# A decoder layer on one core: keys and values prepared one batch ahead, the experts' w2 product in seven block products, and three tiles for the decays

## The chip, the cores and the metric

The kernel is one program on one core of a Trainium2 chip, with float32 data throughout. The metric is the device time of one launch, in microseconds (us): 5657.23 as the median of three runs, 5656.19 to 5658.22. Five engines work side by side, each in its own order: PE multiplies matrices (a weight load and a multiplication by turns), DVE does elementwise work, reductions and scans, ACT does functions and scaled copies, POOL does the rest and issues the indirect transfers, and SP issues nearly all other transfers (DMA). SBUF is the on-chip memory, PSUM holds matmul results, and DRAM is the memory outside the core. An engine or SP that waits holds up what stands behind it in its own queue.

## The reference, cut to what matters

The input x has 8 batches of 512 tokens of 512 values. Three blocks follow each other, each as layernorm(x + block(x)).

```python
# 1. state space block: 1024 channels, 16 states a channel, along the tokens t
h[t] = exp(A * dt[t]) * h[t-1] + dt[t] * B[t] * x_main[t]
y[t] = sum over states of h[t] * C[t]
out  = ((y + x_main * D) * silu(z)) @ out_proj_w + x
# 2. cross attention, 16 heads of 32; keys and values come from ctx, not from x
q, k, v = x @ Wq.T + bq, ctx @ Wk.T + bk, ctx @ Wv.T + bv
out = softmax(q k.T / sqrt(32)) v @ Wo.T + bo
# 3. 32 experts, the best 4 for each token, 640 places each, and a shared expert
xe = xp[buf_tok].reshape(E, cap, DIM)
h = silu(xe @ w1) * (xe @ w3)
out = (h @ w2) * buf_w
y = zeros.at[buf_tok].add(out)
z = silu(xf @ sw1) * (xf @ sw3) @ sw2
return y + z
```

## The kernel before, in words

The program has three parts: `layers` (blocks 1 and 2, the shared expert and the choice of experts), `experts`, and `finish` (the last layernorm). The framework sets the order of every engine's instructions when the program is built, by their order in the source as a priority and by what it takes to be ready, and it places the waits. The order in the trace is therefore not the order of the source everywhere: an expert's weight sums, for instance, stand one expert earlier in DVE's order.

**The scan.** `layers` goes through 16 chunks: 8 batches of two chunks of 256 tokens. A chunk has 32 steps, each with 4 states of one group of 128 rows. In a step ACT writes the decays exp(A dt) into one of two tiles (`decays`, L434, four ACTIVATE), ahead by one step; `carry` (L440) puts the last state in front; DVE makes dt B x (L446), runs the recurrence (L450), and multiplies by C (`collect`, L467); PE sums over the states into `py` (L471). h has four buffers. The broadcasts of B and C, `bc`, come by SP's queue (L378) into four buffers. With the steps go the projections of the next chunk (L302) and the output projection of the last (`back`, L500), whose result is normed, written to DRAM as x1d (L512), and read again by `fetch` (L668).

**Beside the scan.** Attention and shared expert of the batch before are a list of small pieces with weights (`units(b)`), taken one by one between the steps of the scan, as a budget over both chunks allows. A piece issues its matmuls and leaves a second half (the copy out of PSUM) to be issued with the following piece. In batch 0 there are no such pieces; the pieces of batch 7 come after the last chunk, alone. A list begins with the loads of Wv, of ctx into `cT` and of the mask; then come four `values` products, copied by ACT into the value tile `va` (L690); four `keys` products, which DVE adds bk to and masks into `kT` (L702); the transposes of x1 (`flip`, L676); four `queries` products (L712). For every pair of heads `spread` copies rows of qT and kT into operand tiles (L722, L723). After attention come the output projection, a layernorm, the gate, the shared expert (`hidden`, `shared`) and the scatter of token rows to the experts' places (`send`, L638). Matmuls of this part have two PSUM tiles (tag `mm`) and weights two buffers (tag `wa`). Four large tiles are shared by tag: s1 holds x1T, then x2t; s2 holds cT, then attT; s3 holds qT, then hT; s4 holds kT, then x2T. Small rows of 512 values use two buffers with the tag `row`. During the first two chunks SP also clears the experts' token buffer, 43 MB in 32 transfers.

**The experts.** For each expert `load` fetches xe (1362.5 KB) and w1, w3, w2 (1024 KB each) into two buffers each. `hidden` computes silu(xe w1) * (xe w3) for two groups of 128 columns (r = 0, 1) and two halves of 320 tokens; its products with w1 and w3 are made as seven block products instead of eight, from sums of weight blocks (`sums_w`) and of token blocks (`sums_x`) that DVE makes (L1127, L1144 to L1147). `give` multiplies a tile of 128 tokens of hT by w2 (L1218: four matmuls of 128x512), ACT scales the result by the token's weight into y (L1222), and POOL adds it into `based` in DRAM by an indirect transfer (L1223). Five tiles make the 640 tokens; between them stand the transposes of the next expert's tokens (`flip`, L1136) and their copy (L1137). Each indirect transfer waits until the one before has landed, and the x load of the next expert but one into the same buffer waits for the last of them. PSUM has three tiles with the tag h, two with h2, one for transposes and two for L1218.

A matmul of 128x128 by N float32 columns is two records of N columns in the profile.

## Time and profile before

| | |
|---|---|
| median of 3 runs | 5657.23 us |
| profiled execution | 5660.41 us, of which the span from first to last instruction is 5658.7 us |
| PE, DVE, ACT, POOL busy in the span | 87%, 73%, 45%, 9% |
| granted clock of PE | 0.937 on average |
| scan with what goes beside it | to about 3724 us |
| last batch's attention and shared expert | 3724 to 3985 us |
| experts | 3985 to 5602 us, 49.5 us each |
| final layernorm | to the end |

In a row by stage the first pair of figures is the window and its length, then busy microseconds and instruction counts of PE, PEld (weight loads), DVE, ACT and POOL, the granted clock as a share of full speed, the mean share of time that the DMA engines worked, and GB/s. In a row of waits stand the engine and line that waited, what it waited for, the sum in us, how often, and the longest. In a row of the timeline stand the start, the duration of the merged group, engine and line, and in brackets the idle time before it with what ended it.

### The profile page before, as it was taken

The numbers are of one execution on the slowest core, as the hardware profiler recorded it, in microseconds if no ns is written. First come the engines' busy times: TensorE is split into PE (matmuls) and PEld (weight loads), VectorE is DVE, ScalarE is ACT, GpSimd is POOL, SyncE is SP. The second block draws the span as 40 slices with busy tenths as digits, with TensorE's granted clock in tenths as the row PEclk, the third lists the DMA queues.
The fourth block names the chain that finished last, engine by engine and source line by source line (L and its number), as shares of the span: only waits on it lengthen the run. The fifth ranks groups of instructions, "written<-read, shape, count | busy, mean of one in ns | idle before, by whom it ended". The sixth has DMA issues, their size and how long they took to land. (4 is left out here: it accounts for less than half of the span.)

```text
span 5658.7 us, 57578 instructions
## 1 busy us (share of the span) xinstructions
PE 4933.6 (87%) x18984; PEld 2576.2 (46%) x18984; DVE 4107.3 (73%) x5290; ACT 2548.5 (45%) x5347; POOL 525.2 (9%) x424
## 2 busy tenths in 40 slices
PE   5658889888988988988898898889899999999994
PEld 3334344334434433434443443333566666666662
DVE  5998988989899898898999999834444444444443
ACT  4454565654655456565465646513122222222223
POOL 0000001002000200200200020010211111111111
PEclk8778999999999999999999999999999999999997
DMA  7675345335433634544443363331544444444444
GB/s 205 192 225 176 96 127 164 110 116 158 137 105 108 188 95 127 162 112 117 159 136 105 110 194 94 107 110 43 159 123 115 118 125 115 119 117 123 115 118 137
DMA packets 484635, 744.49 MB, mean 132 GB/s; under 512 B 68170, under 2 KB 200810, under 8 KB 484336
## 3 DMA queue, kind: packets, MB, share of 16 engines
q1 hardware_dynamic: 446832, 655.52, 38.1%
q0 software_dynamic: 33280, 76.90, 7.1%
q10 hardware_dynamic: 4224, 8.39, 0.4%
q8 instruction: 150, 2.46, 0.2%
q14 instruction: 149, 1.22, 0.1%
HBM read 491.91 MB, written 148.28 MB: 113 GB/s over the span
## 5 line engine op out<-in xcount | busy, mean ns | idle before, releaser
L434 ACT ACTIVATE l_da<-both,l_aneg 128x256 f32<-128x256 f32 x2048 | 894.0, 499 | 837.6 <-DVE h L450 795.6
L450 DVE TENSOR_TENSOR_SCAN h<-l_da,h 128x1028 f32<-128x1028 f32 x512 | 1172.4, 2295 | 55.0 <-ACT h L440 28.7
L471 PE MATMUL py<-h,l_twice 128*64 128x256 f32 x4096 | 632.4, 421 | 225.9 <-DVE h L467 225.7
L446 DVE TENSOR_TENSOR h<-both,bc 128x1024 f32<-128x1024 f32 x512 | 619.5, 1217 | 125.2 <-PE py L471 58.3
L467 DVE TENSOR_TENSOR h<-h,bc 128x1024 f32<-128x1024 f32 x512 | 624.1, 1221 | 6.3 <-DVE l_state L452 0.3
L1218 PE MATMUL po<-w,hT 128*128 128x512 f32 x1280 | 575.1, 592 | 0.0
L471 PEld LDWEIGHTS py<-h,l_twice 128*64 128x64 f32 x4096 | 297.9, 147 | 588.1 <-DVE h L467 262.0
L735 PE MATMUL ps_s<-l_ka,l_qa 64*128 64x512 f32 x1024 | 316.9, 698 | 140.8 <-DVE mx L737 140.6
L1152 PE MATMUL ps_h<-xT,w 128*128 128x320 f32 x1536 | 436.7, 434 | 0.0
L1173 DVE TENSOR_TENSOR hT<-ps_h,p 128x320 f32<-128x320 f32 x128 | 63.0, 492 | 443.4 <-PE ps_h L1152 443.4
L1223 POOL DMA_INDIRECT based<-y,xe x160 | 252.2, 1576 | 1358.8 <-ACT y L1222 828.6
L737 DVE TENSOR_REDUCE mx<-ps_s 128x2 f32<-128x1024 f32 x256 | 310.9, 1217 | 81.6 <-PE ps_s L735 81.0
L1222 ACT ACTIVATE y<-po,xe 128x512 f32<-128x512 f32 x160 | 110.0, 688 | 551.7 <-PE po L1218 542.6
L1152 PEld LDWEIGHTS ps_h<-xT,w 128*128 128x128 f32 x1536 | 292.9, 191 | 131.8 <-issue 15.8
L1218 PEld LDWEIGHTS po<-w,hT 128*128 128x128 f32 x1280 | 231.1, 190 | 231.6 <-issue 224.1
L761 PE MATMUL ps_t<-l_qa,l_ka 64*128 64x512 f32 x1024 | 303.3, 655 | 12.9 <-ACT eT L765 9.0
L765 ACT ACTIVATE eT<-ps_t 128x1024 f32<-128x1024 f32 x256 | 258.9, 1013 | 108.3 <-PE ps_t L761 108.0
L777 PE MATMUL po<-eT,l_va 128*64 128x512 f32 x1024 | 278.8, 623 | 21.2 <-ACT raw L789 18.1
L1152 PE MATMUL ps_h<-t,s 128*128 128x320 f32 x1024 | 286.2, 432 | 0.0
L682 PE MATMUL ps_p<-x2T,wa 128*128 128x512 f32 x512 | 249.6, 639 | 21.1 <-DVE hT L852 19.2
L500 PE MATMUL po<-wm,zs 128*128 128x512 f32 x512 | 241.6, 623 | 21.5 <-DMA wm<-in_out_proj_w 21.5
L302 PE MATMUL ps_z<-xnT,wm 128*128 128x256 f32 x1024 | 241.6, 389 | 12.7 <-DMA wm<-in_in_proj_w 12.7
(205 smaller groups left out, 6695.3 us busy)
## 6 DMA issues: line engine op xcount, KB each, us to landing
bc<-scr SPq DMA_DIRECT2D x1024, 128.0 KB
w<-in_w SPq DMA_DIRECT2D x96, 1024.0 KB
wm<-in_in_proj_w SPq DMA_DIRECT2D x128, 512.0 KB
xbuf<-zero SPq DMA_DIRECT2D x32, 1362.5 KB
xe<-xbuf SPq DMA_DIRECT2D x32, 1362.5 KB
both<-dt SPq DMA_DIRECT2D x256, 128.0 KB
both<-dtx SPq DMA_DIRECT2D x256, 128.0 KB
wm<-in_out_proj_w SPq DMA_DIRECT2D x64, 512.0 KB
```

Source lines behind the costliest of these rows:

```text
L434: nc.scalar.activation(da[:, n, 1:], dt[:, c % 2, j, :], AF.Exp, scale=aneg[:, c, j, g, m : m + 1])
L446: nc.vector.tensor_tensor(steps, dtx[:, c % 2].unsqueeze(2).to_broadcast([P, 2, NG // 2, T]), bc[0], ALU.mult)
L450: nc.vector.tensor_tensor_scan(flat, da.rearrange("p n t -> p (n t)"), flat, 0.0, ALU.mult, ALU.add)
L467: nc.vector.tensor_tensor(steps, steps, bc[1], ALU.mult)
L471: nc.tensor.matmul(py[j * HP : (j + 1) * HP, c % 2, :], twice, h[:, j * 2 + m, 1:], start=False, stop=(s == (NST // NG - 1, NG // 2 - 1, 1)),)
L735: nc.tensor.matmul(ps[:, j, :], qa[r, lt * P : (lt + 1) * P], ka[r, :], start=True, stop=True)
L737: return lambda: nc.vector.tensor_reduce(mx[:, lt, :].unsqueeze(2), ps, AX.X, ALU.max) and None
L761: nc.tensor.matmul(ps[:, j, :], ka[r, kc * P : (kc + 1) * P], qa[r, :], start=True, stop=True)
L765: nc.scalar.activation(eT, ps, AF.Exp)
L777: nc.tensor.matmul(po[j * 2 * HD : (j + 1) * 2 * HD, :], va[:, kc, i, j * HD : (j + 2) * HD], eT[:, j, :], start=(kc == 0), stop=(kc == SC ...
L1152: nc.tensor.matmul(ps, w[:, n, r * P : (r + 1) * P], x[:, n, :], start=not more and n == 0, stop=n == 1, skip_group_check=more,)
L1218: nc.tensor.matmul(po, got["hT"][:, ic, j * P : (j + 1) * P], got["w2"][:, ic, :], start=(ic == 0), stop=(ic == DC - 1))
```

## The change

Three things are done.

First, keys and values move out of `units(b)` into a list of their own, `sources(b)`. The list for batch b+1 is run inside `units(b)` (its last two key products behind the start of `units(b)`), so during the scan of batch b+1; the list for batch 0 is run beside the scan of batch 0, which had nothing beside it; and `units(7)`, behind the last chunk, has none. The results are kept in DRAM (`kept`): a value or key product is copied into a `row` tile and stored by SP; `units` later loads the values into `va` by eight transfers in runs of 128 bytes, and `spread` loads key rows from DRAM instead of from kT. The tag s4 is gone; x2T goes into s3 and hT into s2. Wq is loaded at the first key product or, for the last batch, at the start of `units`.

Second, `give` now computes four of the five token tiles as two by two blocks (token halves of 256, column halves of 256, contraction halves of 256) with seven block products instead of eight; the fifth tile is computed as before. DVE makes four sums of w2's blocks (`sums_w2`, beside the first group of `hidden`) and four of hT's blocks (one of them in place). Partial results are scaled by the token's weight on ACT (`keep`), and DVE combines them (`use`). The transposes of the next expert are issued at five places between the products (`between`). hT, its sums and w2's sums have one buffer each, and y has seven.

Third, the decays have three tiles in turn instead of two.

Besides, two gate constants (`early`, `first`) are kept once and broadcast instead of stored four times, and two gate temporaries use a `row` tile.

```diff
-    das = [cp.tile([P, NG, T + 1], F32, name=f"l_da{i}") for i in range(2)]
+    das = [cp.tile([P, NG, T + 1], F32, name=f"l_da{i}") for i in range(3)]
...
+    early = cp.tile([P, E], F32, name="l_early")
...
+    early = early.unsqueeze(1).to_broadcast([P, SC, E])
...
+        both = p3.tile([P, D], F32, tag="row", name="g_eq").rearrange("p (n j g h) -> p n j g h", n=2, j=SC, g=G)
+        eq, gt = both[:, 0], both[:, 1]
...
+    kept = {}
+    def sources(b):
+        st, todo = {}, []
+        def begin():
             load("Wv")
             st["cT"] = cT = quad("s2", "cT")
             nc.sync.dma_start(cT, rows(a["ctx"][b]))
             st["mk"] = mk = p1.tile([P, S], U8, tag="mk", name="mk")
             nc.sync.dma_start(mk, a["mask"][b : b + 1, :].to_broadcast([P, S]))
+            kept[b] = [dp.tile([S, D], F32, tag="vd", name="vd"), dp.tile([D, S], F32, tag="kd", name="kd")]
+        def values(pc):
+            if pc == 0:
+                load("Wk")
+            w, cT = loaded["Wv"], st["cT"]
+            ps = dense(lambda dc: cT[:, dc, pc * P : (pc + 1) * P], lambda dc: w[:, dc, :])
+            def put():
+                v = p3.tile([P, D], F32, tag="row", name="v")
+                nc.scalar.copy(v, ps)
+                nc.sync.dma_start(kept[b][0][pc * P : (pc + 1) * P, :], v)
+            return put
+        def keys(oc):
+            if oc == 0 and b:
+                load("Wq")
+            w, cT = loaded["Wk"], st["cT"]
+            ps = dense(lambda dc: w[:, dc, oc * P : (oc + 1) * P], lambda dc: cT[:, dc, :])
+            def put():
+                k = p3.tile([P, D], F32, tag="row", name="k")
+                nc.vector.scalar_tensor_tensor(k, ps, bk[:, oc : oc + 1], st["mk"], ALU.add, ALU.mult)
+                nc.sync.dma_start(kept[b][1][oc * P : (oc + 1) * P, :], k)
+            return put
+        todo.append((0, begin, False))
+        for j in range(SC):
+            todo.append((3.4, lambda j=j: values(j), False))
+        for j in range(DC):
+            todo.append((3.4, lambda j=j: keys(j), False))
+        return todo
+    def dense(lhs, rhs):
+        ps = psm.tile([P, S], F32, tag="mm", name="ps_p")
+        for dc in range(DC):
+            nc.tensor.matmul(ps, lhs(dc), rhs(dc), start=(dc == 0), stop=(dc == DC - 1))
+        return ps
+    def units(b):
+        st = {}
+        todo = []
+        def begin():
+            if b == B - 1:
+                load("Wq")
             st["x1T"] = quad("s1", "x1T")
+            vd, st["kd"] = kept.pop(b)
+            for pc in range(SC):
+                for j in range(2):
+                    nc.sync.dma_start(
+                        va[:, pc, :, 2 * j * HD : (2 * j + 1) * HD],
+                        vd[pc * P : (pc + 1) * P, :].rearrange("p (i j d) -> p i j d", j=2, d=HD)[:, :, j, :],
+                    )
...
-        def values(pc):
-            if pc == 0:
-                load("Wk")
-            w, cT = loaded["Wv"], st["cT"]
-            ps = dense(lambda dc: cT[:, dc, pc * P : (pc + 1) * P], lambda dc: w[:, dc, :])
-            return lambda: nc.scalar.copy(
-                va[:, pc].rearrange("p i (j d) -> p i j d", d=HD)[:, :, 0:3:2, :],
-                ps.rearrange("p (i j d) -> p i j d", j=2, d=HD),
-            ) and None
-        def keys(oc):
-            if oc == 0:
-                load("Wq")
-                st["kT"] = quad("s4", "kT")
-            w, cT = loaded["Wk"], st["cT"]
-            ps = dense(lambda dc: w[:, dc, oc * P : (oc + 1) * P], lambda dc: cT[:, dc, :])
-            return lambda: nc.vector.scalar_tensor_tensor(
-                st["kT"][:, oc, :], ps, bk[:, oc : oc + 1], st["mk"], ALU.add, ALU.mult
-            ) and None
...
-                nc.sync.dma_start(ka[r1 : r1 + HD, :], st["kT"][r0 : r0 + HD, i // 2, :])
+                h0 = (2 * i + j) * HD
+                nc.sync.dma_start(ka[r1 : r1 + HD, :], st["kd"][h0 : h0 + HD, :])
...
-                st["x2T"] = quad("s4", "x2T")
+                st["x2T"] = quad("s3", "x2T")
...
-                st["hT"] = quad("s3", "hT")
+                st["hT"] = quad("s2", "hT")
...
-        for j in range(SC):
-            add(3.4, values, j)
-        for j in range(DC):
-            add(3.4, keys, j)
-            if j == 2:
-                add(0, fetch, 0)
+        more = sources(b + 1) if b + 1 < B else []
+        todo += more[:-2]
+        add(0, begin)
+        add(0, fetch, 0)
+        todo += more[-2:]
...
-        if t == 0 and b:
-            side, spent = units(b - 1), 0.0
+        if t == 0:
+            side, spent = units(b - 1) if b else sources(0), 0.0
...
-                decays(2 * nq + ni, ng, (f if k + 1 < len(steps) else nf)["ready", nq][0], das[(n + 1) % 2])
-            scan(t, 2 * q + ci, g, f["ready", q][1], bc, das[n % 2], h)
+                decays(2 * nq + ni, ng, (f if k + 1 < len(steps) else nf)["ready", nq][0], das[(n + 1) % 3])
+            scan(t, 2 * q + ci, g, f["ready", q][1], bc, das[n % 3], h)
...
+    def BW(w, j, k):
+        return w[:, 2 * j : 2 * j + 2, k * FH : (k + 1) * FH]
...
-        s1, s2, s4 = (wp.tile([P, 2, FH], F32, tag=f"{n}s{i}", name="s") for i in (1, 2, 4))
+        s1, s2, s4 = (wp.tile([P, 2, FH], F32, tag=f"{n}s{i}", name="s", bufs=1 if n == "hT" else 2) for i in (1, 2, 4))
...
+    def sums_w2(got):
+        w = got["w2"]
+        got["t2"] = t1, t2, t3, t4 = [wp.tile([P, 2, FH], F32, tag=f"w2t{i}", name="t", bufs=1) for i in range(4)]
+        for o, x, y in (
+            (t1, BW(w, 0, 1), BW(w, 0, 0)),
+            (t2, BW(w, 1, 1), t1),
+            (t3, BW(w, 1, 1), BW(w, 0, 1)),
+            (t4, BW(w, 1, 0), t2),
+        ):
+            nc.vector.tensor_tensor(o, x, y, ALU.subtract)
+            yield
...
-    def give(e, got, j):
-        xe = got["x"]
+    def give(e, got, side):
+        xe, hT, w2 = got["x"], got["hT"], got["w2"]
+        t1, t2, t3, t4 = got["t2"]
+        both = range(2)
+        ys = [p2.tile([P, D], F32, tag="y", name="y", bufs=CJ + 2) for j in range(CJ)]
+        def weight(j):
+            return xe[:, j, D + e : D + e + 1]
+        def keep(ps, r, tag, j):
+            v = p2.tile([P, HALF], F32, tag=f"{tag}{r}", name=tag)[:, 0:FH]
+            nc.scalar.activation(v, ps, AF.Identity, scale=weight(j))
+            return v
+        def use(j, k, ps, more):
+            nc.vector.scalar_tensor_tensor(ys[j][:, k * FH : (k + 1) * FH], ps, weight(j), more, ALU.mult, ALU.add)
+        def put(j):
+            nc.gpsimd.indirect_dma_start(
+                out=based,
+                out_offset=bass.IndirectOffsetOnAxis(ap=xe.bitcast(I32)[:, j, D + E :], axis=0),
+                in_=ys[j],
+                in_offset=None,
+                bounds_check=N + P - 1,
+                compute_op=ALU.add,
+            )
+        for _ in sums_w(got, "hT"):
+            pass
+        s1, s2, s3, s4 = got["hT", "s"]
+        next(side, None)
+        xs, p1, pu, p5 = [], [], [], []
+        for r in both:
+            xs.append(psx.tile([P, HALF], F32, tag="h", name="ps_o")[:, 0:FH])
+            product(xs[r], A(hT, 0, 0), r, BW(w2, 0, 0))
+            p1.append(keep(xs[r], r, "p1", r))
+        j = CJ - 1
         po = pso.tile([P, D], F32, tag="po", name="po")
         for ic in range(DC):
-            nc.tensor.matmul(
-                po, got["hT"][:, ic, j * P : (j + 1) * P], got["w2"][:, ic, :], start=(ic == 0), stop=(ic == DC - 1)
-            )
-        y = p2.tile([P, D], F32, tag="y", name="y", bufs=CJ + 1)
-        nc.scalar.activation(y, po, AF.Identity, scale=xe[:, j, D + e : D + e + 1])
-        nc.gpsimd.indirect_dma_start(
-            out=based,
-            out_offset=bass.IndirectOffsetOnAxis(ap=xe.bitcast(I32)[:, j, D + E :], axis=0),
-            in_=y,
-            in_offset=None,
-            bounds_check=N + P - 1,
-            compute_op=ALU.add,
-        )
+            nc.tensor.matmul(po, hT[:, ic, j * P : (j + 1) * P], w2[:, ic, :], start=(ic == 0), stop=(ic == DC - 1))
+        nc.scalar.activation(ys[j], po, AF.Identity, scale=weight(j))
+        put(j)
+        next(side, None)
+        for r in both:
+            ps = psy.tile([P, HALF], F32, tag="h2", name="ps_o")[:, 0:FH]
+            product(ps, A(hT, 0, 1), r, BW(w2, 1, 0))
+            use(r, 0, ps, p1[r])
+        for r in both:
+            product(xs[r], s2, r, t2, more=True)
+            pu.append(keep(xs[r], r, "pu", r))
+        next(side, None)
+        zs = []
+        for r in both:
+            zs.append(psy.tile([P, HALF], F32, tag="h2", name="ps_o")[:, 0:FH])
+            product(zs[r], s1, r, t1)
+            p5.append(keep(zs[r], r, "p5", 2 + r))
+        for r in both:
+            product(xs[r], s3, r, t3, more=True)
+            use(2 + r, 1, xs[r], p5[r])
+        next(side, None)
+        for r in both:
+            product(zs[r], s4, r, BW(w2, 1, 1), more=True)
+            use(r, 1, zs[r], pu[r])
+            put(r)
+        next(side, None)
+        for r in both:
+            product(xs[r], A(hT, 1, 1), r, t4, more=True)
+            nc.scalar.activation(ys[2 + r][:, 0:FH], xs[r], AF.Identity, scale=weight(2 + r))
+            put(2 + r)
+    def between(nxt):
+        sums = sums_w(nxt, "w3")
+        for j in range(CJ):
+            flip(nxt, j)
+            if j == CJ - 1:
+                sums_x(nxt)
+            next(sums, None)
+            yield
...
-        got["hT"] = p2.tile([P, DC, CAP], F32, tag="hT", name="hT")
+        got["hT"] = p2.tile([P, DC, CAP], F32, tag="hT", name="hT", bufs=1)
         for r in range(2):
-            hidden(got, r, sums_w(nxt, "w1") if nxt and r else iter(()))
-        side = sums_w(nxt, "w3") if nxt else iter(())
-        for n, j in enumerate(reversed(range(CJ))):
-            if nxt:
-                flip(nxt, n)
-                if n == CJ - 1:
-                    sums_x(nxt)
-            next(side, None)
-            give(e, got, j)
-        for _ in side:
-            pass
+            hidden(got, r, sums_w2(got) if r == 0 else sums_w(nxt, "w1") if nxt else iter(()))
+        give(e, got, between(nxt) if nxt else iter(()))
```

## The prediction

> **What bounds the kernel now.** I read the page's slices first, then busy time by stage, then the waits inside each stage, then the order of instructions at the places the change touches.
>
> The page's slices: 26 of heavy VectorE work, a short stretch, then twelve in which VectorE is at 4 tenths and PE at 9 or more.
>
> ```profile
> PE   5658889888988988988898898889899999999994
> DVE  5998988989899898898999999834444444444443
> ```
>
> Busy time by stage (columns: PE, PEld, DVE, ACT, POOL, granted clock, DMA share, GB/s): batch 0's scan, a later batch's, the last batch's attention alone, the experts.
>
> ```profile
> 100.00:530.00 430.00, 282.12 (x1169) 152.38 (x1168) 405.18 (x414) 232.50 (x548) 17.14 (x12) 0.77 0.66 197
> 1900.00:2360.00 460.00, 400.52 (x1640) 188.13 (x1639) 420.50 (x493) 259.94 (x550) 37.26 (x29) 0.94 0.44 130
> 3724.00:3985.00 261.00, 230.52 (x740) 90.64 (x739) 86.15 (x155) 67.88 (x90) 23.34 (x27) 0.94 0.25 81
> 4036.00:5570.00 1534.00, 1534.00 (x5329) 955.23 (x5328) 645.60 (x1139) 379.54 (x775) 244.50 (x155) 1.00 0.45 116
> ```
>
> The reader is to see three limits: DVE in batch 0 (94%, PE 66%), DVE at 91% with PE close behind (87%) in the later batches, PE alone in the tail and in the experts, where it never stops and the clock is whole.
>
> What DVE waited for between 100 and 3724 us:
>
> ```profile
> DVE h L446 <- PE py L471: 58.3, 25, 7.8
> DVE zs L483 <- PE py L471: 38.6, 19, 4.3
> DVE h L450 <- ACT h L440: 28.7, 17, 2.9
> DVE xs L336 <- ACT xs L328: 22.2, 16, 3.1
> DVE h L450 <- ACT l_da L434: 11.4, 14, 2.4
> DVE h L446 <- DMA bc<-scr: 8.6, 7, 1.3
> ```
>
> The decays (L434) end only 11.4 us of DVE's idle time there, though ACT itself stands 795.6 us before them waiting for the scan.
>
> PE in one expert's down-projection and behind the last scan chunk:
>
> ```profile
> 4828.16 3.60 PE L1218 MATMUL po<-w,hT 128*128 128x512 f32 x8
> 4831.60 0.60 PE L1136 MATMUL ps_t<-e_ident,xe 128*128 128x128 f32 x4
> 4832.03 3.60 PE L1218 MATMUL po<-w,hT 128*128 128x512 f32 x8
> ...
> 3735.81 9.80 PE L500 MATMUL po<-wm,zs 128*128 128x512 f32 x16 [4.92 <-DMA wm<-in_out_proj_w]
> 3745.44 13.90 PE L682 MATMUL ps_p<-wa,cT 128*128 128x512 f32 x32
> 3759.18 13.90 PE L682 MATMUL ps_p<-cT,wa 128*128 128x512 f32 x32
> ...
> 3782.01 15.76 PE L682 MATMUL ps_p<-x1T,wa 128*128 128x512 f32 x32 [0.68 <-ACT x1T L677]
> ```
>
> A matmul is two records (8 records are four matmuls). The tail's keys and values stand on PE's path, 3745.4 to 3772.9, but at the place where the last rows of x1 are normed, written and read back.
>
> **The change part by part.** The sum is made against the profiled execution, 5660.4 us (span 5658.7 and 1.7 around it), 3.2 above the median of 5657.2.
>
> *w2 as seven products.* Removed: four of five tiles. From one L1218 start to the next is 3.87 us, four transposes take 0.44 (4831.60 to 4832.03), so a tile costs 3.43 and four 13.72. Added: 7 products x 2 row halves x 2 matmuls x 2 records = 56 records of 256 columns. Bounds: 128x320 records in this stage follow each other by 0.2695 us (16 of them from 4847.09 to the next group's start at 4851.40: 4.31), which for 256 columns gives 0.2155 and 12.07 us; the x16 groups of 256 columns at L302 in the scan stage need 3.65 from start to next start, 0.228 each, 12.77 us. The saving is 1.65 or 0.95 us an expert. I take 1.65, since the new records stand in the same unbroken stream as the 320-column ones: 32 x 1.65 = **-52.8** (bound -30.4).
>
> The Trainium skill's "Perfetto Trace Analysis", section Matmuls, speaks against this: larger matmuls are more efficient than smaller ones. Its "TensorE: Matmul & The Clock Gate", section "Wait — 56ns, not 53.3ns?", puts the fixed cost at about 2.5 ns a matmul; 24 more records an expert would then be 0.06 us, 2 us in all (an estimate from that page), and the term -51. The rows above already show the fixed part to be small.
>
> DVE gets eight sums (128x512, 0.685 us) and six combinations (128x256 with PSUM, at most the 0.49 of a 128x320): 8.4 us, on 20.8 of 49.5 now; 29 of 48 still leaves room. ACT swaps four 0.69 evictions for eight of at most 0.43. Is a sum late? The last piece of hT is finished 1.1 us after PE leaves the hidden part (4828.00 plus 0.49, against 4827.4); four sums take 2.8 more, and a DVE that first waits for a weight load until 4832.7, as now, has the second sum by +6.7. PE reaches the first product that needs a sum at +7.7 (transposes 0.43, first product 1.7, fifth tile 3.43, transposes 0.43, second product 1.7). Covered by one microsecond; I allow 0.15 us an expert, **+4.8** (ends 0 and 54, where the gain is all gone). hT in one buffer costs nothing: its next writer is 3.5 us behind the next expert's first matmul (4850.59 against 4847.09).
>
> The scattered adds bunch up. They run one behind the other, 5.2 to 6.1 us apart:
>
> ```profile
> 4838.81 1.54 POOL L1223 DMA_INDIRECT based<-y,xe  x1 [4.00 <-DMA based<-y,xe]
> 4844.05 1.54 POOL L1223 DMA_INDIRECT based<-y,xe  x1 [3.70 <-DMA based<-y,xe]
> ```
>
> Now the first is issued 5.4 us into the down-projection and the last lands at about +32. After, one goes at +6.5 and four from +15.5 on, so the last lands at about +36, and only then can the next x load (SP waits for it, at 4810.10 here) be issued; it needs some 6.4 us, done at +42.5, and the transposes ask for it at +47.8. Hidden by 5 us. At the end of the last expert nothing hides it: the last add lands at 34.1 instead of 30.8 (5601.2 less 5570.4), **+3.3**.
>
> *Keys and values a batch ahead, the tail.* 27.5 us of matmuls leave it (-27.5 if nothing follows late). Late next: the rows of x1. The write is issued at 3750.6, lands about 2.5 later (another batch's write frees its buffer so), the read takes about 2.5 to 3, transposes and copies 2.2; the queries start near 3758.6 instead of 3782.0, 23.4 earlier; a colder clock over the gap takes 1.4: **-22**. If the read takes 5.8, as it did here beside a weight load, -19; twice in series, -13.
>
> *Batch 0* gets that work. PE is 34% idle there; DVE is not, and four key combinations of 0.74 us are +3.0. ACT's four copies and the matmuls hide in that idle time. 3 MB more loads and 2 MB of stores on DMA engines 66% busy: 0 to 25 us (5 MB at 197 GB/s). I take **+4** in all, near the low end, as DMA ended only one 9.0 us wait of DVE there.
>
> *The round trip through DRAM, seven batches.* The same matmuls, copies and combinations; new are eight stores and eight value loads a batch; the key loads were there and only change their source. On SP's queue a store waits for its ACT or DVE result; behind it stand the broadcasts (bc) that DVE needs. The nearest row is the split of the attention output: SP waited 83.6 us in 28 times for ACT raw, 3.0 each. 8 x 3.0 x 7 = 168 us if all of it reached DVE; 0 if none. I take **+6**: SP already waits 342 and 289 us for DVE to free those same bc buffers, while DVE waits 8.6 for a bc. The load of cT now waits for the hidden tile's buffer, so for the last shared product (store at 1860.4); the first value product ran at 1890, and 1 MB needs far less than 30 us.
> The values are read back in runs of 128 bytes. Such packets took 11 ns each in this trace, those of 2048 bytes 84: 8192 packets over 16 engines are 5.6 us of DMA a batch, beside scan.
> The Trainium skill's "DMA: Bandwidth & Descriptors", Specifications, speaks against runs under 512 B (no line rate, read-modify-write); these packets moved at half the rate per byte, so the rule holds, and whole rows would save 3 us a batch off the path.
>
> *The third decay tile.* Decays may run while the scan before still reads. It can return what ACT's lateness costs DVE: 11.4 + 28.7 (the carry stands behind blocked decays), at most 62.3 with the convolution's 22.2; nothing of the 96.9 that PE ends. In the other direction, ACT's order changes and copies may slip behind decays: +20 by the same rows. I take **-15**, between, as PE is the usual last one. The constants broadcast instead of stored, and the gate's borrowed row tile, cost nothing: the same DVE instructions, beside scan work.
>
> Sum: -52.8 + 4.8 + 3.3 - 22 + 4 + 6 - 15 = -71.7; 5660.4 - 71.7 = 5588.7; against the median, **5586 us**.
>
> **The rivals.** (1) *Expert gain half eaten*: DVE, fuller by 8.4 us, is late at the border between down-projection and next hidden part (the sums of x end at 4847.74 now, 3.6 us before their first product at 4851.4; after, four transposes end at +15.8, copy and sums take 3.7, the product comes at +21.8, 2.3 to spare and less with other steps between); 0.85 us of PE waiting an expert, 27 us: 5613. For it: six more DVE steps between PE and PSUM. Against: DVE 60% busy, PE 0 idle now. (2) *Slower: stores hold SP's queue.* If each of the eight stores a batch holds the broadcasts 3.0 us and DVE has no cover, 168 - 6 more: 5748. It decides from 72 us, 10 us a batch; for it, SP's strict order and four bc buffers; against, the 8.6. (3) *x late for the transposes.* If the bunched adds take 8 us apart instead of 5.3, the last lands at +47 and x is 5.6 late in 31 experts, +174: 5760; it decides from 2.3 us late, an add pitch of 7.2. Against: 6.1 is the most I saw. (4) *ACT mattered more*: all 62 returned: 5539.
>
> **How the numbers follow.** Forecast 0.58 (own range 5555 to 5610), rival 1 0.16, rival 2 0.11, rival 3 0.06, rival 4 0.09. The range 5535 to 5655 holds the forecast, 1 and 4 and a light form of 2. No change to a measurement is within 0.2%, 11 us. Faster 0.77 (forecast, 1, 4, less a heavy form of 1), same 0.05, slower 0.18 (2, 3 and a little).
>
> **What would show it.** Right: an expert every 47.9 us instead of 49.5; queries of the last batch start 13 us after L500 ends (3745.4) instead of 37; ACT's wait for the scan far under 795.6; DVE's waits for L434 and L440 down. Wrong: PE idle at hT's sums or at the transposes for x in every expert; DVE waiting for bc; batches longer than 457 us. What would make it wrong is a build order in the scan stage that shifts PE's py products later, where 96.9 us already hang on them.

## The result and the profile after

The changed kernel takes 5632.8 us (median of five runs, 5629.2 to 5638.3); the kernel before, run beside it, took 5658.2. The ratio is 0.9951, with a 95% interval from 0.9937 to 0.9965: faster by 25 us, where 72 were forecast. The profiled execution of the changed kernel took 5631.7 us, with a span of 5630.0.

The spans divide at four marks of the two traces: the first scan, the last scan, the first and the last transposes of an expert's tokens.

| stretch | before, us | after, us | difference | forecast |
|---|---|---|---|---|
| start to first scan | 84.9 | 84.2 | -0.7 | 0 |
| batch 0's scans | 351.6 | 362.2 | +10.6 | +4 |
| scans of batches 1 to 7 | 3265.1 | 3292.1 | +27.0 | +6 - 15 = -9 |
| last scan to first expert | 294.3 | 275.2 | -19.1 | -22 |
| first to last expert | 1540.7 | 1491.7 | -49.0 | -52.8 + 4.8 |
| last expert to the end | 122.0 | 124.7 | +2.7 | +3.3 |

Experts, tail and end came as forecast within 3 us. The whole miss lies in the scan stage: +37.6 us, where the forecast had -5.

The page's slices of the changed kernel:

```profile
PE   5667889888888988988888898879899999999994
DVE  5998998899889989989988899864556555555554
```

VectorE is now at 5 tenths in the experts (it was at 4), and the heavy stretch in front is as long as before. Busy time by stage, columns as in the prediction:

```profile
100.00:530.00 430.00, 299.25 (x1198) 154.50 (x1196) 396.79 (x407) 225.74 (x532) 21.10 (x12) 0.80 0.69 209
1900.00:2360.00 460.00, 404.28 (x1652) 193.52 (x1650) 413.00 (x485) 264.88 (x557) 25.99 (x22) 0.93 0.44 131
3760.00:4005.00 245.00, 203.50 (x675) 78.38 (x673) 82.67 (x151) 65.55 (x86) 24.81 (x28) 0.91 0.24 78
4055.00:5540.00 1485.00, 1484.31 (x6074) 1096.43 (x6073) 875.90 (x1573) 412.03 (x899) 242.77 (x155) 1.00 0.47 119
```

In the experts PE still never stops and DVE, busy 59% instead of 42%, has room. In the later batches DVE did less in the same 460 us (413.0 instead of 420.5): it waits more. What for, between 100 and 3760 us:

```profile
DVE h L451 <- ACT h L441: 38.9, 20, 3.4
DVE st L73 <- DMA xt<-in_x: 38.7, 14, 9.6
DVE xs L337 <- ACT xs L329: 33.7, 21, 3.8
DVE dtx L410 <- ACT dtx L406: 27.0, 7, 5.2
DVE mx L766 <- PE ps_s L764: 25.8, 15, 2.2
DVE h L447 <- PE py L472: 21.1, 19, 3.6
...
DVE h L447 <- DMA bc<-scr: 8.3, 7, 1.3
```

Waits have changed places. The wait for py in front of dt B x (L446, now L447) fell from 58.3 to 21.1 us, but those for the carry (28.7 before), for x (13.4), for the convolution (22.2), for dtx (5.2) and for the scores (14.0) rose by 81 us together. The wait for the broadcasts, the one the forecast feared, did not move (8.6 to 8.3).

PE in one expert's down-projection, and in the tail:

```profile
5108.76 3.60 PE L1299 MATMUL po<-w,hT 128*128 128x512 f32 x8
5112.20 0.60 PE L1168 MATMUL ps_t<-e_ident,xe 128*128 128x128 f32 x4
5112.63 1.89 PE L1197 MATMUL ps_o<-w,hT 128*128 128x256 f32 x8
5114.36 1.89 PE L1197 MATMUL ps_o<-t,s 128*128 128x256 f32 x8
...
3771.21 9.75 PE L501 MATMUL po<-wm,zs 128*128 128x512 f32 x16 [4.98 <-DMA wm<-in_out_proj_w]
...
3791.58 1.94 PE L731 MATMUL ps_tr<-l_ident,xr 128*128 128x128 f32 x8 [9.12 <-DMA xr<-x1d]
3794.19 17.07 PE L701 MATMUL ps_p<-x1T,wa 128*128 128x512 f32 x32 [0.68 <-ACT x1T L732]
```

A product of eight records of 256 columns takes 1.73 us (5112.63 to 5114.36), so seven take 12.1; the forecast had 12.07. In the tail the queries now start 13.2 us behind the output projection (3780.96 to 3794.19); the forecast said 13.

### The profile page after: what moved, and what is told of

Same layout as the page of the kernel before. It is cut to its first block, busy times and chain, and to the rows that moved or that the text cites. A ratio compares the mean times of both kernels' runs of the same rounds, so it can differ in the third digit from the quotient of the medians.

```text
span 5630.0 us, 60426 instructions
## 1 busy us (share of the span) xinstructions
PE 4906.6 (87%) x19752; PEld 2732.5 (49%) x19752; DVE 4354.2 (77%) x5738; ACT 2585.2 (46%) x5480; POOL 549.1 (10%) x425
## 5 line engine op out<-in xcount | busy, mean ns | idle before, releaser
L447 DVE TENSOR_TENSOR h<-both,bc 128x1024 f32<-128x1024 f32 x512 | 619.2, 1216 | 83.4 <-DMA both<-dtx 27.6
L764 PE MATMUL ps_s<-l_ka,l_qa 64*128 64x512 f32 x1024 | 333.1, 709 | 147.3 <-DVE mx L766 147.1
L766 DVE TENSOR_REDUCE mx<-ps_s 128x2 f32<-128x1024 f32 x256 | 310.3, 1217 | 97.2 <-PE ps_s L764 95.8
L806 PE MATMUL po<-eT,l_va 128*64 128x512 f32 x1024 | 279.5, 624 | 12.6 <-ACT eT L794 8.0
L639 POOL DMA_INDIRECT xbuf<-x2t,dest x128 | 217.2, 1697 | 626.2 <-DVE dest L633 587.9
L501 PE MATMUL po<-wm,zs 128*128 128x512 f32 x512 | 249.7, 641 | 10.2 <-DMA wm<-in_out_proj_w 5.8
L303 PE MATMUL ps_x<-xnT,wm 128*128 128x256 f32 x1024 | 241.8, 390 | 3.0 <-DMA wm<-in_in_proj_w 1.6
L303 PEld LDWEIGHTS ps_z<-xnT,wm 128*128 128x128 f32 x1024 | 198.4, 198 | 86.1 <-issue 27.4
```

The source lines that it names most:

```text
L303: nc.tensor.matmul(ps[:, i, :], w[:, dc, i * P : (i + 1) * P], f["xnT"][:, dc, :], start=(dc == 0), stop=(dc == DC - 1),)
L447: nc.vector.tensor_tensor(steps, dtx[:, c % 2].unsqueeze(2).to_broadcast([P, 2, NG // 2, T]), bc[0], ALU.mult)
L764: nc.tensor.matmul(ps[:, j, :], qa[r, lt * P : (lt + 1) * P], ka[r, :], start=True, stop=True)
L766: return lambda: nc.vector.tensor_reduce(mx[:, lt, :].unsqueeze(2), ps, AX.X, ALU.max) and None
L806: nc.tensor.matmul(po[j * 2 * HD : (j + 1) * 2 * HD, :], va[:, kc, i, j * HD : (j + 2) * HD], eT[:, j, :], start=(kc == 0), stop=(kc == SC ...
```

## The experiments

All kernels below were timed in three rounds against the kernel before; ratios are to it. A "step" is one of the 32 scan steps of a chunk, counted from 0 and timed from the start of its scan to the next one; a "first half" is the first of a batch's two chunks. Lengths of steps and halves are means over batches 2 to 7 of the profiled execution, worked out from the start times of the scans. The median of the kernel before lay between 5657 and 5663 us from one group of runs to another, so times of different groups compare to within some 5 us.

### One part at a time

Two decay tiles, all else as changed; only w2 in seven products; and w2 with the third tile but keys and values as before. (To make room the third one lets the mask share a tile, keeps one gate constant fewer and reuses a gate temporary.) Theory A was the forecast's: the third tile gives 15. Theory B: its new order on ACT costs the scan. Theory C: it does nothing.

```diff
# e1, against the changed kernel
-    das = [cp.tile([P, NG, T + 1], F32, name=f"l_da{i}") for i in range(3)]
+    das = [cp.tile([P, NG, T + 1], F32, name=f"l_da{i}") for i in range(2)]
...
-            scan(t, 2 * q + ci, g, f["ready", q][1], bc, das[n % 3], h)
+            scan(t, 2 * q + ci, g, f["ready", q][1], bc, das[n % 2], h)
# e2: the kernel before, with experts() of the changed kernel
# e3, against e2: the lines of e1 the other way round
```

> The changed kernel with two decay tiles in turn, as before; keys and values ahead and the seven w2 products stay. Between the first and the last scan the changed kernel takes 3654 us where the kernel before takes 3617, 37 more, and I forecast 9 less (third tile -15, round trip through DRAM +6) after batch 0. Theory A (the third tile gives its 15, keys and values cost the rest): this run is slower than the changed kernel by 15, about 5648 us. Theory B (the third tile's new order of ACT costs the scan stage some 25, keys and values only batch 0's 10): this run is faster, about 5608 us. Theory C (the third tile gives nothing): 5633 us. The experts stay at 47.9 us each in all three.

> The kernel before with the seven w2 products alone. The experts' stage should be the changed kernel's (47.9 us an expert, 49 us less between the transposes of the first and of the last expert) and the scan and the tail those of before: 5658 - 49 + 3 (last adds land later) = 5612 us by every theory, which is 21 under the changed kernel and would make the other two parts together a loss of 21. If the two parts help through something that the stages don't show, 5640 or more.

> The seven w2 products and three decay tiles on the kernel before, keys and values not ahead (room is made by letting the mask share the tile of the softmax sums, by dropping one gate constant for a multiply-add, and by reusing one gate temporary). Theory A: 15 under the run with the products alone, 5597 us. Theory B: 25 above it, 5637. Theory C: equal to it, 5612. The share of the scan's waits of ACT for the scan (795.6 us before, 485.9 in the changed kernel) should fall in all three.

| kernel | time, us | ratio, 95% | batch 0 | batches 1 to 7 | steps 20 to 24 of a first half |
|---|---|---|---|---|---|
| w2 alone | 5619.0 | 0.9931 (0.9910 to 0.9951) | 351.4 | 3260.9 | 35.8 |
| w2, third tile | 5643.0 | 0.9979 (0.9967 to 0.9991) | 351.4 | 3291.7 | 39.7 |
| w2, keys and values ahead | 5618.5 | 0.9932 (0.9916 to 0.9949) | 361.7 | 3279.5 | 35.7 |
| all three (the change) | 5632.8 | 0.9951 (0.9937 to 0.9965) | 362.2 | 3292.1 | 39.6 |

Theory A falls. w2 alone was expected at 5612 us and took 5619.0 (5605.8 to 5623.4 in its runs). The third tile costs 24 us alone, near theory B's figure, and 14 beside the other parts, between the figures of B and C. Keys and values ahead bring nothing at all: against w2 alone the stretch behind the last scan is 25 us shorter (275.0 instead of 300.1), and that is given back in batch 0 (+10.3) and in batches 1 to 7 (+18.6 by the spans). And the third tile's loss has a place: steps 20 to 24 of the first halves, 3.9 us a batch, 23 us in six; the second halves did not grow.

### The third tile: which instruction stands in front

DVE at that place in batch 3's first half, first with two tiles and then with three (start, duration, operation, idle time before it and what ended it):

```profile
1530.74 1.22 DVE L468 TENSOR_TENSOR h<-h,bc 128x1024 f32<-128x1024 f32 x1
1531.88 1.22 DVE L766 TENSOR_REDUCE mx<-ps_s 128x2 f32<-128x1024 f32 x1
1533.02 2.46 DVE L337 SCALAR_TENSOR_TENSOR xs<-xp,l_cw,xs 128x256 f32<-128x256 f32 x6
1535.39 1.22 DVE L766 TENSOR_REDUCE mx<-ps_s 128x2 f32<-128x1024 f32 x1
...
1537.65 1.22 DVE L766 TENSOR_REDUCE mx<-ps_s 128x2 f32<-128x1024 f32 x1
...
1539.39 1.22 DVE L766 TENSOR_REDUCE mx<-ps_s 128x2 f32<-128x1024 f32 x1
...
1541.12 1.21 DVE L766 TENSOR_REDUCE mx<-ps_s 128x2 f32<-128x1024 f32 x1
1542.26 0.68 DVE L412 TENSOR_TENSOR dt<-dt,l 128x512 f32<-128x512 f32 x1
1542.85 2.29 DVE L451 TENSOR_TENSOR_SCAN h<-l_da,h 128x1028 f32<-128x1028 f32 x1
```

```profile
1532.99 1.23 DVE L468 TENSOR_TENSOR h<-h,bc 128x1024 f32<-128x1024 f32 x1
1534.13 2.46 DVE L337 SCALAR_TENSOR_TENSOR xs<-xp,l_cw,xs 128x256 f32<-128x256 f32 x6
1536.51 2.35 DVE L766 TENSOR_REDUCE mx<-ps_s 128x2 f32<-128x1024 f32 x2
1538.77 1.22 DVE L447 TENSOR_TENSOR h<-both,bc 128x1024 f32<-128x1024 f32 x1
1540.09 2.30 DVE L451 TENSOR_TENSOR_SCAN h<-l_da,h 128x1028 f32<-128x1028 f32 x1
1542.50 1.23 DVE L766 TENSOR_REDUCE mx<-ps_s 128x2 f32<-128x1024 f32 x1
...
1544.24 1.22 DVE L766 TENSOR_REDUCE mx<-ps_s 128x2 f32<-128x1024 f32 x1
...
1547.95 1.22 DVE L766 TENSOR_REDUCE mx<-ps_s 128x2 f32<-128x1024 f32 x1 [1.90 <-PE ps_s L764]
...
1563.21 2.30 DVE L451 TENSOR_TENSOR_SCAN h<-l_da,h 128x1028 f32<-128x1028 f32 x1 [3.42 <-ACT h L441]
```

With two tiles a score reduction (L766) comes first, then the six multiply-adds of a convolution, then four more reductions, then the scan. With three, the multiply-adds stand in front of the first reduction, and the scan in front of the last three (the expectations below count two). PE waits for these reductions, first with two tiles and then with three:

```profile
1533.15 0.27 PE L773 MATMUL ps_m<-l_ident,mx 128*2 128x128 f32 x1 [1.21 <-DVE mx L766]
```

```profile
1537.78 0.37 PE L773 MATMUL ps_m<-l_ident,mx 128*2 128x128 f32 x1 [4.18 <-DVE mx L766]
```

Counted from step 20's scan (1521.41 and 1523.66) the product starts 2.4 us later. PE's score products behind it are late, DVE soon finds no scores (1.90 us idle), and a later scan waits 3.4 us for its carry instead of 2.0.

Three runs tell the causes apart. In the first the decays of step 23 go back into the tile of step 21, in the first halves only. In the second all tiles stay, and the scan alone is queued on DVE behind the reductions it overtook. In the third the multiply-adds go behind their reduction as well.

```diff
# e5_two_at_23
+    use.append(use[m - 2] if m % (2 * len(steps)) == 23 else (use[m - 1] + 1) % 3)
-            scan(t, 2 * q + ci, g, f["ready", q][1], bc, das[n % 3], h)
+            scan(t, 2 * q + ci, g, f["ready", q][1], bc, das[use[n]], h)
# e6_scan_behind: the scan of step 22, first halves of batches 1 to 7
+            if rest:
+                with tc.issue_after(reduced[-5].ins):
+                    rest()
# e9_taps_behind: e6 and, for the third convolution of a second half,
+                    with tc.issue_after(reduced[-1].ins):
+                        taps()
```

> The changed kernel with three decay tiles, but in the first half of every batch the decays of step 23 go into the tile of step 21, as with two tiles; all other steps rotate through three. Reason for it: between the kernels with two and with three tiles, steps 20 to 24 of a batch's first half are the stretch that grew (35.7 us to 39.5, in six or seven batches), and the second halves did not grow. Theory D (the cost of the third tile is one change of order at that stretch, in which a scan stands on DVE ahead of two score reductions): those steps return to 35.7 us, the time to 5633 - 23 = 5610. Theory E (the cost is ACT's order at the same stretch, the negated maxima ahead of the logarithm): the same 5610, this run does not part D and E. Theory F (carry copies behind hoisted decays, spread over all steps): 5633, within 4.

> The changed kernel with three decay tiles throughout; only the scan of step 22 in the first half of batches 1 to 7 is queued on DVE behind the second of the score reductions that it had overtaken. DVE's order of scans, reductions and decay arithmetic there is then that of the kernel with two tiles, while ACT keeps the order of the changed kernel (negated maxima ahead of the logarithm). Theory D (the overtaking scan): steps 20 to 24 return to about 36 us, the time to 5610. Theory E (ACT's order): 5630 to 5633. Theory F (spread carries): 5633, within 4.

> The changed kernel with three decay tiles throughout. In the first half of batches 1 to 7 two things are queued later on DVE: the scan of step 22 behind the second score reduction that it had overtaken, and the six multiply-adds of the third convolution behind the score reduction that they had overtaken. DVE's order in steps 20 to 24 is then that of the kernel with two tiles, though the decays still come a step earlier. Theory G (with a third tile ACT is free earlier, serves the convolution 4 us sooner, and the convolution's multiply-adds and then the scan stand in front of score reductions, whose PSUM buffers PE waits for; the run with the scan alone moved gave back 1.2 of the 3.8 us): steps 20 to 24 return from 38.3 to 35.7 us, the time to 5619, within 4. If something else in the third tile's order costs the remaining 2.6 us a batch: they stay at 38.3 and the time at 5631.

| kernel | time, us | ratio, 95% | steps 20 to 24 |
|---|---|---|---|
| three tiles (the change) | 5632.8 | 0.9951 (0.9937 to 0.9965) | 39.6 |
| three, but step 23 in the tile of step 21 | 5618.9 | 0.9930 (0.9903 to 0.9956) | 35.7 |
| three, scan behind the reductions | 5631.4 | 0.9953 (0.9937 to 0.9969) | 38.3 |
| three, scan and multiply-adds behind | 5619.4 | 0.9922 (0.9906 to 0.9939) | 35.7 |

The place is the cause: with it mended the time is that of two tiles (5618.5). Theory F, carries spread over all steps, falls with the first run. Theory D, the scan, explains 1.3 of 3.9 us; theory G, the multiply-adds, the other 2.6. Theory E (ACT's negated maxima ahead of the logarithm) isn't needed: in the second run that order still stood, and the logarithm's followers on ACT were done 0.4 us before the late reduction began. It isn't excluded by a run of its own, since with the multiply-adds moved that order swapped back too. I had expected 5610 of the first run, 23 us for the six batches, and got 14: the rest of the three-tile kernel is not faster than the one with two, though the forecast had believed so.

The way there leads over ACT. Because decays are done a step earlier, ACT copies the convolution's input 3.8 us sooner after step 20's scan, and an order made at build time takes what is ready first.

The Trainium skill's "Perfetto Trace Analysis", section "Optimization Strategy", says that a gap which repeats on the engine that should be saturated can mean too few buffers. DVE's waits for decays and carry were such gaps, and here the further buffer made the kernel slower; the measured 14 us decide.

### Keys and values ahead: SP's queue

Stores of keys and values issued by POOL's queue instead of SP's: with three tiles; with two tiles; with two and three tiles and the value loads moved too; and with the mended three tiles.

```diff
# e4 (three tiles), e11 (two tiles)
-                nc.sync.dma_start(kept[b][0][pc * P : (pc + 1) * P, :], v)
+                nc.gpsimd.dma_start(kept[b][0][pc * P : (pc + 1) * P, :], v)
-                nc.sync.dma_start(kept[b][1][oc * P : (oc + 1) * P, :], k)
+                nc.gpsimd.dma_start(kept[b][1][oc * P : (oc + 1) * P, :], k)
# e7 (two tiles), e10 (three), e12 (three, as e5): also the loads of va by nc.gpsimd
# e8: two tiles, stores on SP, only the load of x by POOL
-        nc.sync.dma_start(xt, a["x"][b, t * T : (t + 1) * T, :].rearrange("(j p) d -> p j d", p=P))
+        nc.gpsimd.dma_start(xt, a["x"][b, t * T : (t + 1) * T, :].rearrange("(j p) d -> p j d", p=P))
```

> The changed kernel with the eight stores a batch of keys and values issued by POOL instead of SP; value loads stay on SP. Rival 2 of the prediction in a light form (stores that wait for ACT or DVE hold the broadcasts behind them on SP): the scan stage loses most of its extra 37 us, 5605 to 5612 us. If SP's order is not the cause: within 5 us of 5633.

> The changed kernel with two decay tiles, the stores of keys and values and the loads of the values into the 65-column tiles issued by POOL instead of SP. If the 7 us of the run with the stores on POOL and the 14 us of the run with two tiles add up: 5618.5 - 7 = 5611, and down to 5607 if the value loads held SP too. If the two overlap in the same waits: 5618, within 4.

> The changed kernel with two decay tiles, and only the load of x (one per half batch) issued by POOL instead of SP. DVE waited 36 us for x in the run with two tiles, and 15 us in the run without keys and values ahead. If x is late because its load stands behind stores and loads of keys and values in SP's queue: the wait falls to about 15 us and the time to 5618.5 - 16 = 5602. If x is late because the transfers themselves are slower beside them, or the wait only moves to another place: 5618, within 4.

> The changed kernel, three decay tiles, with the stores of keys and values and the loads of the values issued by POOL. If the third tile's 14 us do not depend on SP's queue: 5600 + 14 = 5614, steps 20 to 24 of the first halves at 39.5 us. If they were a matter of late transfers too: 5600, within 5.

> The changed kernel with two decay tiles and only the stores of keys and values issued by POOL; the value loads stay on SP. The run with both on POOL gave 5600 against 5618.5. If the stores alone held SP: 5600, within 4. If stores and loads share it as the run with three tiles had it (7 us for the stores): 5611. If the loads are all of it: 5618.

> The changed kernel with stores of keys and values and loads of the values issued by POOL, and three decay tiles with the one exception of step 23 in a batch's first half, which takes the tile of the step before the last. If the third tile without its bad place is worth what the forecast gave it: 5600 - 15 = 5585. If, as the run with SP's queue as it was showed, it is worth nothing once that place is mended: 5600, within 4.

| kernel | time, us | ratio, 95% | longer query products, of 7 batches |
|---|---|---|---|
| three tiles, stores on SP (the change) | 5632.8 | 0.9951 (0.9937 to 0.9965) | 6 |
| three tiles, stores on POOL | 5625.7 | 0.9944 (0.9928 to 0.9961) | 0 |
| three tiles, stores and loads on POOL | 5625.8 | 0.9934 (0.9917 to 0.9950) | 1 |
| two tiles, stores on SP | 5618.5 | 0.9932 (0.9916 to 0.9949) | 7 |
| two tiles, stores on POOL | 5602.7 | 0.9901 (0.9884 to 0.9917) | 3 |
| two tiles, stores and loads on POOL | 5599.8 | 0.9896 (0.9868 to 0.9924) | 2 |
| mended three tiles, stores and loads on POOL | 5603.0 | 0.9896 (0.9880 to 0.9913) | 2 |
| two tiles, x on POOL | 5643.3 | 0.9970 (0.9958 to 0.9982) | 6 |

The stores on SP cost 16 us with two tiles and 7 with three, the value loads at most 3 more. The mended third tile is worth nothing here either (5603.0 against 5599.8). Several figures were missed. Three tiles with the stores on POOL, 5625.7, lies between the figures of its two theories, and 5599.8 is 11 us under the sum of the two gains. With stores and loads on POOL the third tile costs 26 us (5625.8 against 5599.8), not 14 or 0; mending it there returns 23, which is 3.9 us in six batches. Moving the load of x was a miss of both theories: 25 us slower, and DVE's wait for x rose from 36.1 to 47.2 us. POOL stood 695 us before those loads, waiting for the x1 store that frees the tile, with its other work behind; how this makes 25 us stays open.

The last column leads on. It counts, over the seven batches whose attention runs beside a scan, those in which, in the profiled execution, the first two query products took 8.5 to 10.2 us; in the others they took 7.13. In the kernels before and with w2 alone it is 2 of 7. The count alone does not set the time: with three tiles and 0 or 1 such places it stays at 5626. One such place, with two tiles and stores on SP (PE, SP, then windows around it, with the columns of the rows by stage):

```profile
1493.35 0.65 PE L460 MATMUL py<-xs,l_ident 128*64 128x256 f32 x4 [1.07 <-DVE zs L484]
1496.81 1.70 PE L731 MATMUL ps_tr<-l_ident,xr 128*128 128x128 f32 x8 [2.81 <-DMA xr<-x1d]
1499.18 9.51 PE L701 MATMUL ps_p<-x1T,wa 128*128 128x512 f32 x16 [0.68 <-ACT x1T L732]
1508.53 3.62 PE L303 MATMUL ps_x<-xnT,wm 128*128 128x256 f32 x16
```

```profile
1489.21 2.55 SPq L424 DMA_DIRECT2D both<-dtx  x4
1491.86 0.54 SPq L687 DMA_DIRECT2D kd<-k  x1
1492.50 0.88 SPq L723 DMA_DIRECT2D xr<-x1d  x2
```

```profile
1493.77:1497.18 3.41, 0.60 (x8) 0.40 (x4) 3.41 (x3) 1.04 (x5) 1.11 (x1) 1.00 0.89 295
1497.18:1500.60 3.42, 2.75 (x9) 1.57 (x8) 3.42 (x4) 2.64 (x6) 0.00 (x0) 0.50 1.06 374
1500.60:1504.01 3.41, 3.41 (x5) 1.33 (x4) 3.41 (x4) 1.73 (x5) 0.00 (x0) 0.50 0.43 110
1504.01:1507.42 3.41, 3.41 (x9) 1.51 (x8) 3.41 (x5) 2.12 (x5) 0.00 (x0) 1.00 0.06 15
```

A key's store stands before the read of x1's rows. PE waits 2.81 us for them, and its granted clock falls to 0.50. In this trace the clock changes only on a grid of 3.41 us, and the windows above are cut along it: in the first PE worked 0.60 us, and the clock was 0.50 in the next two. Between 90 and 3600 us the clock stayed whole after 766 such windows, all with over 1.5 us of PE work, and fell after 97, half of them with at most 1.14. So the queries take 9.5 us, and the convolution's product behind them, for which DVE waits, is late by the wait and the clock together. The same place with the stores on POOL:

```profile
1489.44 0.63 PE L731 MATMUL ps_tr<-l_ident,xr 128*128 128x128 f32 x4 [1.45 <-DMA xr<-x1d]
...
1491.91 7.13 PE L701 MATMUL ps_p<-x1T,wa 128*128 128x512 f32 x16 [0.68 <-ACT x1T L732]
1498.88 3.62 PE L303 MATMUL ps_x<-xnT,wm 128*128 128x256 f32 x16
```

The stores are only a part of this. PE's wait for rows of x1 in batches 1 to 7 is 19.7 us in all with the stores on SP, 11.8 with them on POOL and 3.6 with w2 alone. Counted from step 12's scan, the read for the third transposes is issued after 28.1, 27.5 and 25.7 us (means over batches 2 to 7). So about half of the longer wait came with keys and values ahead even where their stores stood elsewhere.

The Trainium skill's "TensorE: Matmul & The Clock Gate", section "What's actually happening", has this rule: after an idle window of about 3.4 us the clock gate passes half the pulses, until the array has been busy for such a window, and the windows run freely. The 0.50 here agrees, and so does the grid of 3.41 us; windows that run freely also fit that the same place is slow in some batches and not in others. An idle window in the strict sense is not needed here: PE worked 0.60 us in it, and its longest pause, 2.81 us, was shorter than the window; the measurement decides.

### Filling PE's gap instead

If the gap in front of the queries is the cost, and not SP's queue as such, work of PE put into the gap must bring it back with the stores left where they are. The last key product of the next batch moves from before the four transposes of x1 to between the second and the third.

```diff
# e13 (two tiles, stores on SP), e14 (two tiles, stores and loads on POOL), e15 (three tiles, stores on SP)
-        todo += more[-2:]
+        todo += more[-2:-1]
         for j in range(SC):
+            if j == 2:
+                todo += more[-1:]
             add(0.5, flip, j)
```

> The changed kernel with two decay tiles and the stores on SP; only the place of the last key product of the next batch moves, from before the transposes of x1 to between the second and the third of the four. In the run with two tiles PE waited 2.8 us for the rows of x1 before the third transpose, its granted clock then fell to 0.50 for some 5 us, and the first two query products took 8.6 to 9.5 us in all seven batches that are covered by scans (7.13 where the clock was whole: 4 of 7 batches with the stores on POOL). Theory H (keys and values ahead take work from in front of the queries, PE waits there for x1, and the lower clock after that wait makes the queries and the convolution behind them late): with a 3.5 us product in the gap the query products take 7.13 us in at least five of seven batches, a first half of a batch is 3.6 us shorter, the time 5618.5 - 7 x 2 to 3.6 = 5593 to 5604. Theory I (the stores hold SP, and the clock only goes along with it): 5618, within 4.

> The same move of the last key product, with the stores of keys and values and the loads of the values issued by POOL. That kernel without the move took 5600 and had two of seven batches with the longer query products. Theory H: at most 2 x 3.6 us are left, 5593 to 5600. Theory I: 5600, within 4.

> The changed kernel as it is, three decay tiles and stores on SP, with one thing moved: the last key product of the next batch from before the transposes of x1 to between the second and the third. If the gap in front of the queries and the third tile's order in steps 20 to 24 are two separate costs: the query products take 7.13 us in at least five of seven batches, steps 20 to 24 of the first halves stay near 39.5 us, and the time is 5632.8 - 40 = 5593 (the 40 us that the same move gave with two tiles). If the third tile's order costs more where the queries come earlier: 5600 to 5605. If the two are one cost, already gone with the gap: 5579, within 4.

| kernel | time, us | ratio, 95% | longer query products | steps 15 to 20 | steps 20 to 24 |
|---|---|---|---|---|---|
| two tiles, stores on SP | 5618.5 | 0.9932 (0.9916 to 0.9949) | 7 | 37.7 | 35.7 |
| the same, key product moved | 5578.6 | 0.9858 (0.9838 to 0.9877) | 0 | 32.8 | 35.7 |
| moved, stores and loads on POOL | 5576.4 | 0.9853 (0.9834 to 0.9873) | 0 | 32.8 | 35.7 |
| three tiles, key product moved | 5613.7 | 0.9915 (0.9899 to 0.9932) | 0 | 32.8 | 39.7 |

The same place in the first of them:

```profile
1473.00 3.60 PE L701 MATMUL ps_p<-cT,wa 128*128 128x512 f32 x8
1476.44 0.60 PE L731 MATMUL ps_tr<-l_ident,xr 128*128 128x128 f32 x4
1476.97 1.94 PE L472 MATMUL py<-h,l_twice 128*64 128x256 f32 x14
1478.84 0.65 PE L731 MATMUL ps_tr<-l_ident,xr 128*128 128x128 f32 x4
...
1481.15 7.13 PE L701 MATMUL ps_p<-x1T,wa 128*128 128x512 f32 x16
```

No transpose waits for x1, every query pair takes 7.13 us, and the queries' steps are 4.9 us shorter a batch. Theory H holds as to the place, and its size was too small: 40 us instead of 14 to 25, of which 37 lie in the seven first halves. The wait itself (2.8 us a batch) went as well as the slow clock (2.4), which fits. With stores and loads on POOL the move gave 23 us, where H allowed at most 7 and theory I none; 12 of the 23 lie in the first halves, and the rest is not placed. After the move SP's queue hardly matters any more: 5576.4 against 5578.6 us is within the spread of the runs. So what was lost stood in front of PE's queries and not, as forecast, in DVE's wait for broadcasts.

The move did two things at once. There are two tiles for rows of x1, so the third rows are read only when the first transposes are done; these now stand earlier, and the read is issued 17.7 us after step 12's scan instead of 28.1. Whether the earlier read or the work put into the gap ended the wait, no run here separates.

With three tiles the same move gave 19 us and not 40; my first figure, 5593, was a miss of 21, and the other two, 5600 to 5605 and 5579, were missed as well. The stretch of steps 20 to 24 keeps its 39.7 us, so the two are separate costs, but they do not add: the third tile costs 14 us beside the gap and 35 without it. Of the 37 us between the two profiled scan stages 24 lie in steps 20 to 24 and 10 in step 7 of the first halves (20.1 to 21.8 us). Why step 7 grew stays open.

## Why the prediction was wrong, by its own steps

**w2 as seven products: right.** -52.8 + 4.8 were forecast, -49.0 came. The 256-column records cost what the 320-column rows had said (0.216 us a record), the sums are not late, an expert takes 47.9 us, as forecast, in all but two cases (48.5 and 48.8). The late adds at the end: +3.3 forecast, +2.7 measured.

**The tail: right.** -22 against -19.1. From the store of x1's last rows to the queries it is 8.2 us instead of 31.4, so they start 23.2 us earlier by this count, for 23.4 forecast. Counted from the last scan it is 24.7, and behind their start 5.6 us were lost again; the queries themselves took 17.07 us instead of 15.76, near the 1.4 that the forecast had for a colder clock.

**The third tile: the step that failed most.** "It can return what ACT's lateness costs DVE: 11.4 + 28.7 ... I take -15, between, as PE is the usual last one." Measured: +14 in this kernel, a miss of 29 us. The wait for decays did fall, from 11.4 to 5.7 us, but nothing was gained by it even with the bad place mended. The upper end, +20, was in the text, with the wrong mechanism: copies slipping behind decays. What happened is that ACT got free earlier, served the convolution earlier, and so put six multiply-adds and a scan ahead of score reductions for which PE waits: steps 20 to 24 of a first half took 39.6 us instead of 35.7, and 35.7 again with that order mended. The forecast read who waits for ACT; it had to read who waits for DVE. The text's last warning, "a build order in the scan stage that shifts PE's py products later", named the right kind of cause and the wrong product: DVE's wait for py before dt B x fell (58.3 to 21.1 us), its wait for the scores rose (14.0 to 25.8).

**Batch 0: too cheap.** +4 forecast, +10.6 measured, within its ends. DVE's idle time there rose by 6.7 us, beside the +3.0 of key combinations that the forecast had. With two tiles and the stores on POOL batch 0 is 2.6 us shorter (359.1 against 361.7).

**The round trip through DRAM: right resource, wrong victim.** +6 forecast; batches 1 to 7 grew by 18.6 us when keys and values moved ahead (w2 alone against w2 with keys and values ahead), or 14.4 against the kernel before. By steps of a first half, 0 to 11 got 3.5 us shorter a batch, and 12 to 19, where x1 is read and the queries begin, 4.9 longer (52.0 to 56.9); with the key product moved they take 52.6. The forecast priced how long a store on SP holds a broadcast, and DVE's wait for broadcasts stayed at 8.3 us. Instead the read of x1's rows came late, in part by the stores, PE ran dry before the queries, and its clock fell. Rival 2 had "stores hold SP's queue", but with the same victim and 168 us; nothing of that size came.

So -71.7 becomes -28.5 by the spans. There the third tile counts 12.6 us in batches 1 to 7 (3292.1 against 3279.5) instead of -15, a miss of 28; the round trip 14.4 instead of 6, a miss of 8; batch 0 a miss of 7; and the other terms differ by 1 together. The forecast's sum was reachable: with the third tile out and one key product moved, the kernel takes 5578.6 us, and 5576.4 with the stores and value loads on POOL, the fastest here: 0.9853 of the time before (0.9834 to 0.9873). Part of that is not owed to the change, since the kernel before had the same gap in two of seven batches.

## What to carry to other kernels

A buffer more lets its writer run earlier, and where a program's order is fixed at build time by what is ready, everything behind that writer is reordered: before counting the gain, ask which instruction now overtakes which on the bound engine, and who waits for the one overtaken. When work is moved out of a stage, look at what the engine does just before the work that remains: a gap of 3 us in front of a group of matrix products cost itself and then a slow clock here, and moving work that is there anyway into it (which also let the awaited read start earlier) was worth 40 us, against 16 for taking the stores off the queue. Comparing the lengths of equal steps between two traces found both places at once, where the sums of waits only showed that waits had changed places.

## What the runs showed of the hardware

In the traces here the granted clock changed only on a grid of 3.41 us, and it fell without a long pause: after a window in which PE worked 0.60 us it stood at 0.50 for two windows, and one pair of products took 9.5 us instead of 7.1. With a busy PE around it this hardly shows in the mean clock, 0.934 with seven such places and 0.941 with none. A direct transfer of x took POOL 0.76 us to issue and SP 0.37, and eight 256-column records ran at 0.216 us each, no worse than 320-column ones per column.
